# Narrower first weights, their zero subtraction moved into the first block, and their loads put elsewhere

## The chip, the cores and the metric

The kernel runs on one core of a Trainium2 chip. The metric is the device time of one launch in microseconds. A profiled execution gives, beside its time, a trace of every instruction on the engines: TensorE (PE, with its weight loads, PEld, shown apart), VectorE (DVE), ScalarE (ACT) and GpSimd (POOL), and of the DMA queues that SyncE (SP), ACT and POOL fill. Instructions of one engine start in its program order, so one that waits holds up all those behind it.

## The reference

One layer of cross attention and a feed-forward network with weights of integers, for 32 batches of 64 rows of 512 values:

```python
x = x + xattn(layernorm(x), ctx, ctx, Wq, bq, Wk, bk, Wv, bv, Wo, bo)
x = x + ffn(layernorm(x), gate_w, gate_z, gate_s, up_w, up_z, up_s, down_w, down_z, down_s)

def dequantize(imatrix, scales, zeros, group_size, out_dtype):
    rs = jnp.repeat(scales, group_size, axis=0)
    rz = jnp.repeat(zeros, group_size, axis=0)
    return ((imatrix.astype(rs.dtype) - rz.astype(rs.dtype)) * rs).astype(out_dtype)
gate = jax.nn.silu(jnp.dot(x, gate_proj))
up = jnp.dot(x, up_proj)
return jnp.dot(gate * up, down_proj)
```

The attention mixes the 64 rows of a batch (8 heads of 64 columns each, a softmax over 64 scores). The feed-forward network goes from 512 to 1792 columns (gate and up) and back to 512 (down). Its weights are integers from 0 to 15, with a zero and a scale for each group of 128 input rows and each column.

## The kernel before, in words

Two batches make a pair of 128 rows. There are 16 pairs, four to a block, so four blocks of 512 rows. Attention runs on pairs, the feed-forward network on a whole block with the 512 rows as the moving side of each product. Each operand of the feed-forward products is split into a high and a low part (`hTh` and `hTl` for the input, `hh` and `hl` for the hidden values), so that each weight tile is used twice.

**The weights.** `ng`, `nu` and `nd` hold gate, up and down in SBUF for the whole run. They are loaded as 32-bit values by DMAs that POOL issues (`load_wide`, line 265, for gate and up; `load_down`, line 269). Then the zeros are subtracted in place. For gate and up POOL does it with one instruction for each group g of 128 rows (line 302), for down VectorE does it for each 128 rows (line 308). The result is the integers that the products take; scales are applied to the products. The zeros reach SBUF in two steps: `zeros_to_dram` writes them in narrow types to DRAM, and `load_zeros` (line 279) reads them back, copied to all 128 partitions, by three DMAs that SP issues (two for `z16`, which holds gate's and up's zeros, one for `z8`, down's). `z16` and `z8` exist once each, so the load for one chunk has to wait until the subtractions of the chunk before are done.

All this is done in chunks of columns, listed in `wide` (line 166): 512, 512, 512 and 256 of the 1792. `weight_steps` (line 293) is a generator that makes one subtraction at each step, in the order of chunks, and within a chunk first gate and up by turns for g = 0 to 3, then down. It is advanced from two places: four times by the word `integers` in the first block's list, and then a few times in each round of the main loop.

**The first block.** Attention for pairs 0 to 3 is ordered by hand: the string `START` (line 741) lists steps, `0.turn` for the step `turn` of pair 0 and so on, and each engine takes its instructions in this order. The steps of a pair are: `stats`, `scale`, `apply` (layer norm: VectorE, POOL, VectorE), `k`, `q`, `v` and their `_out` forms, `scores`, `highest`, `less`, `exp`, `sums`, `divide` (the softmax; `divide` is POOL's), `turn` and `turn_out` (weights times Wo), `weigh` and `residual` (the attention's output added to x, on VectorE, and x stored), `stats2`, `scale2`, `apply2` (the second layer norm; `scale2` is POOL's), `flip`, `high`, `low` (transposed, then split in `hTh` by ScalarE and `hTl` by VectorE). Words without a number are other work: `gate`, `up` and `down` load the first chunk's weights, `zeros` writes the zeros to DRAM, `broadcast` reads the first chunk's zeros back, `rows` loads the next pairs' x, `quotients` makes ratios of scales (`s_inv`, `s_q`, on VectorE). `behind_products` (line 781) makes the first instruction of what it encloses wait for the TensorE instruction that stands last at that point of the list.

**The main loop** (line 864) goes in 28 rounds for each block. In each round two lanes, one for even and one for odd tiles f of 128 hidden columns, take a step of `gate_up` (line 595: two products for gate and two for up, for one g of one f), `down` of an earlier f takes two steps from round 6 on, and attention of the next block takes a step. Tile f of the first block needs its chunk's integers: f = 0 starts in round 0, f = 1 in round 2, f = 2 in round 4, and so on. Loads of later chunks are issued in rounds 0, 5 and 13 (line 884).

Of the kernel before, what the change touches and what calls it, by code (L numbers as in the profile page):

```python
# [9 lines left out]
F32 = mybir.dt.float32  # L10
F32R = mybir.dt.float32r
I32 = mybir.dt.int32
U8 = mybir.dt.uint8
BF16 = mybir.dt.bfloat16
AF = mybir.ActivationFunctionType
ALU = mybir.AluOpType
# [10 lines left out]
def kernel(  # L27
# [41 lines left out]
    nc = tc.nc  # L69
    B, D, L = x.shape  # L70
    I = gate_w.shape[1]
    P = 128
    NH, HD = 8, L // 8
    KT = L // P
# [16 lines left out]
    z8_dram = dram.tile([FC * L], U8, name="z8_dram")  # L91
# [22 lines left out]
    with ExitStack() as fast:  # L114
        const = fast.enter_context(tc.tile_pool(name="const", bufs=1))
        rows = fast.enter_context(tc.tile_pool(name="rows", bufs=1))
        att = fast.enter_context(tc.tile_pool(name="att", bufs=1))
        blk = fast.enter_context(tc.tile_pool(name="blk", bufs=2))
        zeros = fast.enter_context(tc.tile_pool(name="zeros", bufs=1))
# [43 lines left out]
        bqk = bias[:, : 2 * D].rearrange("p (m d) -> p m d", m=2)  # L163
        bvo = bias[:, 2 * D :]
        CW = 512
        wide = [(c, min(CW, I - c)) for c in range(0, I, CW)]
        w_T = const.tile([P, 4, D], F32, tag="w_T", name="w_T")
        WK, WV, WQ, WO = range(4)

# [95 lines left out]
        def load_wide(w: bass.AP, src: bass.AP, at: int, n: int):  # L265

            newest["POOL"] = nc.gpsimd.dma_start(w[:, :, at : at + n], src[:, :, at : at + n]).ins

        def load_down(at: int, n: int):
            fs = slice(at // P, (at + n) // P)  # L270
            newest["POOL"] = nc.gpsimd.dma_start(nd[:, fs, :], down_rows[:, fs, :]).ins

        def load_weights(at: int, n: int):

            load_wide(ng, gate_rows, at, n)
            load_wide(nu, up_rows, at, n)
            load_down(at, n)

        def load_zeros(at: int, n: int):
            z16 = zeros.tile([P, 2, KT, CW], BF16, tag="z16", name=f"z16_{at}")  # L280
            z8 = zeros.tile([P, KT, CW], U8, tag="z8", name=f"z8_{at}")
            for m in range(2):
                nc.sync.dma_start(
                    z16[:, m, :, :n], z_rows[m, :, at : at + n].partition_broadcast(P)
                )
            nf = n // P
            zd = z8_dram[at // P * L : (at // P + nf) * L]
            nc.sync.dma_start(
                z8[:, :nf, :].rearrange("p f l -> p (f l)"), zd.partition_broadcast(P)
            )  # L290
            return z16, z8

        def weight_steps(zs):

            for i, (at, n) in enumerate(wide):
                if i:
                    zs = load_zeros(at, n)
                z16, z8 = zs
                for g in range(KT):
                    for m, dst in enumerate((ng, nu)):  # L300
                        piece = dst[:, g, at : at + n]
                        nc.gpsimd.tensor_tensor(  # L302
                            piece, piece.bitcast(F32), z16[:, m, g, :n], ALU.subtract
                        )
                        yield
                for i in range(n // P):
                    piece = nd[:, at // P + i, :]
                    nc.vector.tensor_tensor(piece, piece.bitcast(F32), z8[:, i, :], ALU.subtract)
                    yield
# [424 lines left out]
        def chain(*gens):  # L734
# [6 lines left out]
        START = """  # L741
            0.stats 0.scale 0.apply 1.stats projections 1.scale biases
            projections_out 1.apply 2.stats 0.k biases_out 2.scale 3.stats 0.q 1.q
            0.k_out 3.scale 0.q_out 1.k gate zeros 1.q_out 0.scores 1.k_out 2.k
            3.apply 1.scores broadcast 0.highest 2.apply 2.k_out 0.less 0.v
            1.highest 0.exp 2.q 1.less 0.v_out 3.q 0.sums 1.exp 2.v 2.q_out 0.divide
            3.k up 2.v_out 1.sums 2.scores 3.q_out 1.divide 3.k_out 1.v 2.highest
            3.scores 1.v_out 2.less 1.turn 3.highest 2.exp 0.turn rows 3.less
            1.turn_out 2.sums 3.exp 1.weigh 0.turn_out 3.sums 2.divide 3.v
            1.residual 1.stats2 3.divide 0.weigh 3.v_out 2.turn 0.residual 0.stats2  # L750
            1.scale2 3.turn down 2.turn_out 2.weigh 3.turn_out 1.apply2 0.scale2
            scales 2.residual 2.stats2 3.weigh scales_out 1.flip 3.residual 3.stats2
            2.scale2 1.high 0.apply2 3.scale2 integers integers integers integers
            2.apply2 0.flip 1.low 2.flip 3.apply2 0.high quotients 3.flip 2.high
            0.low 3.high 2.low 3.low
        """
        place = places(att)
        with (
# [9 lines left out]
            for p in range(PB):  # L768
                j, i = divmod(p, SET)
# [6 lines left out]

            def first_banks(name: str):
                return ps0.tile([P, 2, CW], F32, tag="s", name=name)

            @contextmanager  # L780
            def behind_products():
# [19 lines left out]
            for step in START.split():  # L801
                if step[0].isdigit():
                    getattr(pairs[int(step[0])], step[2:])()
                elif step == "gate":
                    load_wide(ng, gate_rows, *wide[0])
                elif step == "zeros":
                    zeros_to_dram()
                elif step == "broadcast":
                    with behind_products():
                        weights = weight_steps(load_zeros(*wide[0]))  # L810
                elif step == "up":
                    with behind_products():
                        load_wide(nu, up_rows, *wide[0])
                elif step == "rows":
                    with behind_products():
                        load_rows(PB // SET)
                elif step == "down":
                    with behind_products():
                        load_down(*wide[0])
                elif step == "integers":  # L820
                    next(weights)
                elif step == "quotients":
                    quotients()
                elif step.endswith("_out"):
                    next(halves[step[:-4]], None)
                else:
                    halves[step] = {
                        "projections": lambda: projections(w_nat),
                        "biases": lambda: biases(b_nat),
                        "scales": lambda: scales(s_nat),  # L830
                    }[step]()
                    next(halves[step])
# [30 lines left out]
        with ExitStack():  # L863
            for r in range(NBLK * ROUNDS + LAG):
# [16 lines left out]
                with ExitStack() as behind:  # L881
                    for ins in newest.values():
                        behind.enter_context(tc.issue_after(ins))
                    if r in (0, 5, 13):
                        load_weights(*wide[(0, 5, 13).index(r) + 1])
                    if r < ROUNDS:
                        advance(weights, 2 if r < 4 else 1 + r % 2)
                    else:
                        advance(tops, 1 + (r % 4 == 3))
                    if k in FINISH_AT or k + 2 in FINISH_AT:  # L890
                        advance(finishing)
# [120 lines left out]
```

## Time and profile before

| | us |
|---|---|
| median of 3 runs | 457.89 |
| lowest and highest of them | 454.89, 458.46 |
| the profiled execution, its time | 457.63 |
| the profiled execution, its span in the trace | 455.3 |
| TensorE busy in the span | 413.0 |
| VectorE busy | 330.5 |
| ScalarE busy | 309.3 |
| POOL busy | 280.4 |
| first product of the feed-forward part begins at | 43.85 |

Times within the trace are counted from the start of the span. The profile has several views: busy time of each engine in given stretches ("windows"), the instructions of one engine in order of time (its "timeline"; the columns are start, duration, engine, line, operation, output and inputs, shapes, and in square brackets the idle time before it with what ended it), the chain of waits that ends last, and the packets of the DMA queues in a stretch. Queue q0 holds what POOL issues, q1 what SP issues, q8 and q14 the engines' own instructions. "Issue" as a releaser means that nothing in the profile explains the wait.

### The profile page before, as it was taken

How to read it: one execution, taken by the hardware profiler on the slowest of the kernel's cores; microseconds unless marked ns; L12 is line 12 of the kernel's file. 1: busy time of each engine (PE TensorE's matmuls, PEld its weight loads, DVE VectorE, ACT ScalarE, POOL GpSimd, SP SyncE). 2: the span in 40 equal slices, each digit the busy share in tenths (PEclk: the TensorE clock that was granted, in tenths of full speed). 3: DMA queues.
4: the chain of work that ended last, by engine and by line, in shares of the span. 5: the costliest groups of instructions: out<-in, count | busy, mean ns of one | idle time of the engine just before them, and what ended most of it. 6: DMA issues, size and time to landing. Idle time of an engine off the chain costs nothing.

```text
span 455.3 us, 10322 instructions
## 1 busy us (share of the span) xinstructions
PE 413.0 (91%) x4175; PEld 315.3 (69%) x4175; DVE 330.5 (73%) x510; ACT 309.3 (68%) x473; POOL 280.4 (62%) x293
## 2 busy tenths in 40 slices
PE   4854998998999999999999899999999999999991
PEld 4642564766677776777778577786778888887870
DVE  5959553797979983696869775586869655668672
ACT  2332489665787669686788569785688788777750
POOL 5335749658474487676787676664566887883311
PEclk9988799999999999999999999999999999999996
DMA  6677959436102020141000012130001012100004
GB/s 205 204 246 229 254 188 273 118 100 183 53 26 74 2 93 1 45 141 50 1 23 25 2 48 94 48 94 1 1 1 48 1 47 94 46 1 0 1 2 145
DMA packets 20928, 36.55 MB, mean 80 GB/s; under 512 B 1848, under 2 KB 7432, under 8 KB 20872
## 3 DMA queue, kind: packets, MB, share of 16 engines
q1 hardware_dynamic: 14056, 24.20, 16.2%
q0 software_dynamic: 6208, 11.01, 8.8%
q8 instruction: 35, 0.57, 0.5%
q10 hardware_dynamic: 608, 0.59, 0.4%
q14 instruction: 21, 0.17, 0.1%
HBM read 27.37 MB, written 8.42 MB: 79 GB/s over the span
## 4 chain that ended last, share of the span: by engine, by line
PE 45%; POOL 23%; issue 15%; DVE 10%; ACT 4%; DMA 1%; ACTq 0%; POOLq 0%; DVEq 0%
PE pg L604 11%; PE pu L604 11%; PE pd L649 6%; POOL hl L631 6%; PE pd L652 5%; POOL squares L325 4%; POOL squares L323 4%; POOL hh L630 3%; DVE xn_set L112 2%; DVE y L660 2%; POOL nu L302 2%; POOL q_e_set L488 1%; POOL ng L302 1%; DVE k_eT_set L411 1%; DMA w_nat<-in_L_xattn_Wo_dram 1%
## 5 line engine op out<-in xcount | busy, mean ns | idle before, releaser
L660 DVE SCALAR_TENSOR_TENSOR y<-pd,s_all,y 128x512 f32<-128x512 f32 x204 | 150.1, 743 | 47.6 <-PE pd L652 45.1
L614 ACT ACTIVATE pg<-pg,s_q 128x512 f32<-128x512 f32 x168 | 111.5, 665 | 76.4 <-PE pg L604 75.0
L614 ACT ACTIVATE pu<-pu,s_q 128x512 f32<-128x512 f32 x168 | 110.7, 659 | 4.5 <-PE pu L604 4.4
L604 PE MATMUL pg<-hTh,ng 128*128 128x512 f32 x224 | 91.3, 407 | 6.3 <-POOL nu L302 2.9
L649 PE MATMUL pd<-hh,nd 128*128 128x512 f32 x224 | 93.9, 419 | 1.6 <-DVE y L660 1.1
L630 POOL CAST hh<-h 128x512 fp32r<-128x512 f32 x55 | 35.0, 636 | 93.0 <-DVE h L620 91.2
L604 PE MATMUL pu<-hTh,nu 128*128 128x512 f32 x224 | 90.6, 404 | 0.9 <-POOL nu L302 0.5
L604 PE MATMUL pu<-hTl,nu 128*128 128x512 f32 x224 | 89.3, 399 | 0.0
L604 PE MATMUL pg<-hTl,ng 128*128 128x512 f32 x224 | 89.2, 398 | 0.0
L652 PE MATMUL pd<-hl,nd 128*128 128x512 f32 x224 | 88.7, 397 | 0.0
L631 POOL TENSOR_TENSOR hl<-h,hh 128x512 fp32r<-128x512 f32 x55 | 72.0, 1310 | 4.4
L620 DVE SCALAR_TENSOR_TENSOR h<-pu,s_all,g 128x512 f32<-128x512 f32 x56 | 41.8, 746 | 34.2 <-ACT g L617 27.8
L325 POOL TENSOR_TENSOR squares<-squares 128x512 f32<-128x512 f32 (+1 forms) x46 | 55.1, 1197 | 1.7
L604 PEld LDWEIGHTS pg<-hTh,ng 128*128 128x128 f32 x224 | 42.2, 188 | 20.1 <-ACT pg L614 4.2
L649 PEld LDWEIGHTS pd<-hh,nd 128*128 128x128 f32 x224 | 42.0, 188 | 18.0 <-DVE y L660 4.9
L604 PEld LDWEIGHTS pu<-hTh,nu 128*128 128x128 f32 x224 | 42.3, 189 | 14.0 <-ACT pu L614 2.7
L604 PEld LDWEIGHTS pu<-hTl,nu 128*128 128x128 f32 x224 | 42.3, 189 | 9.7 <-issue 0.4
L604 PEld LDWEIGHTS pg<-hTl,ng 128*128 128x128 f32 x224 | 42.4, 189 | 9.1
L617 ACT ACTIVATE g<-pg,s_all 128x512 f32<-128x512 f32 x56 | 38.7, 692 | 13.9 <-PE pg L604 12.2
L652 PEld LDWEIGHTS pd<-hl,nd 128*128 128x128 f32 x224 | 42.2, 188 | 7.4
L302 POOL TENSOR_TENSOR ng<-ng,z 128x512 fp32r<-128x512 f32 (+1 forms) x16 | 17.0, 1060 | 8.1 <-DMA z<-z_dram 8.1
L302 POOL TENSOR_TENSOR nu<-nu,z 128x512 fp32r<-128x512 f32 (+1 forms) x16 | 17.2, 1072 | 0.0
(290 smaller groups left out, 480.0 us busy)
## 6 DMA issues: line engine op xcount, KB each, us to landing
ng<-in_L_ffn_gate_w_dram POOLq DMA_DIRECT2D x3, 1024.0 KB, 5.9
z<-z_dram SPq DMA_DIRECT2D x6, 512.0 KB
nu<-in_L_ffn_up_w_dram POOLq DMA_DIRECT2D x3, 1024.0 KB, 7.9
c_set<-in_ctx_dram SPq DMA_DIRECT2D x6, 512.0 KB
x<-in_x_dram SPq DMA_DIRECT2D x6, 512.0 KB
nd<-in_L_ffn_down_w_dram POOLq DMA_DIRECT2D x3, 1024.0 KB, 9.6
x_dram<-x SPq DMA_DIRECT2D x6, 512.0 KB
r<-x_dram SPq DMA_DIRECT2D x6, 512.0 KB
```

The costliest lines, as they stand in the source:

```text
L302: nc.gpsimd.tensor_tensor(piece, piece.bitcast(F32), z16[:, m, g, :n], ALU.subtract)
L323: nc.gpsimd.tensor_tensor(square[:, :n], piece, piece, ALU.mult)
L325: nc.gpsimd.tensor_tensor(total[:, :n], total[:, :n], square[:, :n], ALU.add)
L604: nc.tensor.matmul(acc, w[:, g, ts(f, P)], half[:, g, :], start=(g == 0 and half is hi), stop=(g == KT - 1 and half is lo), skip_group_che ...
L614: nc.scalar.activation(acc, acc, AF.Copy, scale=by)
L617: nc.scalar.activation(g_sb, acc, AF.Silu, scale=by)
L620: ins = nc.vector.scalar_tensor_tensor(h_sb, acc, by, g_sb, ALU.mult, ALU.mult)
L630: nc.gpsimd.tensor_copy(hh, h_sb)
L631: ins = nc.gpsimd.tensor_tensor(hl, h_sb, hh.bitcast(F32), ALU.subtract)
L649: nc.tensor.matmul(pd, w, h_hi[t, f], start=(t, f) != LAST, stop=False, skip_group_check=True)
L652: nc.tensor.matmul(pd, w, h_lo[t, f], start=False, stop=True, skip_group_check=True)
L660: ins = nc.vector.scalar_tensor_tensor(y, pd, by, y, ALU.mult, ALU.add)
```

## The change

The first chunk is 256 columns in place of 512, and the narrow chunk is no longer the last; there are still four. All eight subtractions of gate and up for this first chunk are made within the first block's list (eight words `integers` in place of four), gate's four first and then up's, four of them behind pair 3's `divide` and the other four among the `scale2` steps of POOL. The zeros of the first two chunks have buffers of their own (`early_zeros`, one of them from the pool `early`) and are loaded in the list; down's zeros are split off into `load_down_zeros`.

The loads stand elsewhere. The first load of gate moves from behind `1.k` to behind `3.k`, and waits for these products. The first load of up moves from behind `3.k` to behind `0.turn`, beside `rows`. The load of down leaves its place. New words load the second chunk: `more` its zeros (behind pair 3's `turn`), `more_gate` its gate weights (behind pair 1's `scale2`), `more_up` its up weights and down's weights for both chunks (behind pair 3's `scale2`). The main loop then loads the third chunk in round 5 and the fourth in round 13.

```diff
         CW = 512
-        wide = [(c, min(CW, I - c)) for c in range(0, I, CW)]
+        FIRST = 256
+        wide = [(0, FIRST)] + [(c, CW) for c in range(FIRST, I, CW)]
...
-        def load_zeros(at: int, n: int):
-            z16 = zeros.tile([P, 2, KT, CW], BF16, tag="z16", name=f"z16_{at}")
-            z8 = zeros.tile([P, KT, CW], U8, tag="z8", name=f"z8_{at}")
+        def load_zeros(at: int, n: int, pool=zeros):
+
+            z16 = pool.tile([P, 2, KT, n], BF16, tag="z16", name=f"z16_{at}")
             for m in range(2):
-                nc.sync.dma_start(
-                    z16[:, m, :, :n], z_rows[m, :, at : at + n].partition_broadcast(P)
-                )
...
+                nc.sync.dma_start(z16[:, m], z_rows[m, :, at : at + n].partition_broadcast(P))
+            return z16
+
+        def load_down_zeros(at: int, n: int):
+            z8 = zeros.tile([P, KT, CW], U8, tag="z8", name=f"z8_{at}")[:, : n // P, :]
+            zd = z8_dram[at // P * L : (at + n) // P * L]
+            nc.sync.dma_start(z8.rearrange("p f l -> p (f l)"), zd.partition_broadcast(P))
+            return z8
+
+        def weight_steps():
+
+            for at, n in wide:
+                z16 = early_zeros.pop(0) if early_zeros else load_zeros(at, n)
+                z8 = load_down_zeros(at, n)
+                pieces = [(m, g) for g in range(KT) for m in range(2)]
+                for m, g in pieces if at else sorted(pieces):
+                    piece = (ng, nu)[m][:, g, at : at + n]
+                    nc.gpsimd.tensor_tensor(
+                        piece, piece.bitcast(F32), z16[:, m, g, :], ALU.subtract
+                    )
+                    yield
...
-            0.k_out 3.scale 0.q_out 1.k gate zeros 1.q_out 0.scores 1.k_out 2.k
-            3.apply 1.scores broadcast 0.highest 2.apply 2.k_out 0.less 0.v
-            1.highest 0.exp 2.q 1.less 0.v_out 3.q 0.sums 1.exp 2.v 2.q_out 0.divide
-            3.k up 2.v_out 1.sums 2.scores 3.q_out 1.divide 3.k_out 1.v 2.highest
-            3.scores 1.v_out 2.less 1.turn 3.highest 2.exp 0.turn rows 3.less
-            1.turn_out 2.sums 3.exp 1.weigh 0.turn_out 3.sums 2.divide 3.v
-            1.residual 1.stats2 3.divide 0.weigh 3.v_out 2.turn 0.residual 0.stats2
-            1.scale2 3.turn down 2.turn_out 2.weigh 3.turn_out 1.apply2 0.scale2
-            scales 2.residual 2.stats2 3.weigh scales_out 1.flip 3.residual 3.stats2
-            2.scale2 1.high 0.apply2 3.scale2 integers integers integers integers
-            2.apply2 0.flip 1.low 2.flip 3.apply2 0.high quotients 3.flip 2.high
-            0.low 3.high 2.low 3.low
+            0.k_out 3.scale 0.q_out 1.k zeros 1.q_out 0.scores 1.k_out 2.k 3.apply
+            1.scores broadcast 0.highest 2.apply 2.k_out 0.less 0.v 1.highest 0.exp
+            2.q 1.less 0.v_out 3.q 0.sums 1.exp 2.v 2.q_out 0.divide 3.k gate
+            2.v_out 1.sums 2.scores 3.q_out 1.divide 3.k_out 1.v 2.highest 3.scores
+            1.v_out 2.less 1.turn 3.highest 2.exp 0.turn up rows 3.less 1.turn_out
+            2.sums 3.exp 1.weigh 0.turn_out 3.sums 2.divide 3.v 1.residual 1.stats2
+            3.divide integers integers integers integers 0.weigh 3.v_out 2.turn
+            0.residual 0.stats2 1.scale2 more_gate integers 3.turn more 2.turn_out
+            2.weigh 3.turn_out 1.apply2 0.scale2 integers integers scales 2.residual
+            2.stats2 3.weigh scales_out 1.flip 3.residual 3.stats2 2.scale2 integers
+            1.high 0.apply2 3.scale2 more_up 2.apply2 0.flip 1.low 2.flip 3.apply2
+            0.high quotients 3.flip 2.high 0.low 3.high 2.low 3.low
...
+                elif step == "more":
+                    with behind_products():
+                        early_zeros.append(load_zeros(*wide[1]))
+                elif step == "more_gate":
+                    load_wide(ng, gate_rows, *wide[1])
+                elif step == "more_up":
+                    load_wide(nu, up_rows, *wide[1])
+                    load_down(0, wide[1][0] + wide[1][1])
...
-                    if r in (0, 5, 13):
-                        load_weights(*wide[(0, 5, 13).index(r) + 1])
+                    if r in (5, 13):
+                        load_weights(*wide[(5, 13).index(r) + 2])
```

## The prediction, made before the changed kernel had run

> **What bounds the kernel now.** I read the windows of 100 us first. From 120 to 400 us TensorE is busy 77.53 of 80, 97.50 of 100 and 99.05 of 100 us: it is the bound there, and the change takes no matrix product away. The tail (after 435 us) is untouched too. So only the first 100 us can move the time, and there the start, up to the first product of the feed-forward part at 43.85 us, counts one for one, since everything behind it is shifted as a block. The chain of waits, in order of time, shows the hole in it:
>
> ```profile
> 22.10 0.57 PE pe L497 x23
> 22.67 5.15 issue
> 27.82 0.50 PE pe L497 x9
> ...
> 42.97 0.88 issue
> 43.85 0.70 PE pg L604 x2
> ```
>
> `pe` is pair 0's "turn", 32 matmuls with one wait at their head. They break off after 23 and resume 5.15 us later, with no semaphore to wait for ("issue"). What can be missing in the middle of such a run is the instructions. The DMA queues of the second 25 to 26 us (packets, MB, time as a share of the engines) show a block of them landing, between data:
>
> ```profile
> q0 software_dynamic: 150, 0.31, 92.7%
> q1 hardware_dynamic: 36, 0.07, 22.1%
> q8 instruction: 1, 0.02, 6.0%
> ```
>
> The other blocks of q8 before 50 us fall in seconds 11, 16, 28, 32 and 47, each without such a hole. What stood in front of the late one is read from SP's and POOL's timelines: zeros 1.25 MB issued from 17.24 us, up's weights 1 MB from 19.23, the next context 0.5 MB at 20.81. The windows of 2 us give 230 to 392 GB/s from 22 to 28 us.
>
> After the hole VectorE works without a gap until the feed-forward part can start, and its last `hTl` ends 0.1 us before the first `pg` at 43.85 (POOL's fourth subtraction ended at 42.96, so the label POOL on that wait is not the last releaser):
>
> ```profile
> 29.24 0.88 DVE L525 SCALAR_TENSOR_TENSOR x<-po,bias,x 128x256 f32<-128x256 f32 x2 [4.34 <-PE po L513]
> ...
> 33.08 0.54 DVE L112 TENSOR_SCALAR xn_set<-x,mv,rs 128x512 f32<-128x512 f32 x1
> ...
> 38.88 0.84 DVE L112 TENSOR_SCALAR xn_set<-x,mv,rs 128x512 f32<-128x512 f32 x1
> 39.64 1.19 DVE L236 SCALAR_TENSOR_TENSOR s_inv<-s_all 128x84 f32<-128x84 f32 x1
> ...
> 41.87 1.87 DVE L550 TENSOR_TENSOR hTl<-ph,hTh 128x512 fp32r<-128x512 f32 x3
> ```
>
> The 4.34 us of VectorE before 29.24 is all that the hole costs the path, since VectorE had work until 24.89 us. From 44 to 90 us TensorE is busy about nine tenths; ScalarE has no gap from 62.11 to 80.6 us (its timeline, with three table loads of 1.28 us), and POOL waits once, 8.05 us, for zeros (62.82 us).
>
> [...] `xn_set` takes 0.54 us alone and 0.84 beside POOL's subtractions, `s_inv` 1.19 us for 84 columns. [...] Here the clock is 0.50 from 46 to 50 us, and a product takes 0.79 us there against a mean of 0.41.
>
> **The change part by part.** Durations are from the rows above; the zero of the sum is the profiled execution, 457.63 us with a span of 455.3.
>
> *Transfers ahead of the hole.* Gate's first megabyte at 11.08 goes; half of it now stands where up's stood (behind pair 3's k products, 18.4 us). Zeros before the hole shrink from 1.25 to 0.5 MB. From 17.2 to 22.7 us 1.5 MB are queued in place of 2.75. At the 0.3 MB per us of these windows they are through 5 us after the first bytes at 18.5, so at 23.5, and not at 28. [...] I take the hole from 5.15 to 1.0 us; bounds 0 and, if it goes with bytes outstanding at its end, 3.
>
> *VectorE.* It is free at 24.89, so a hole of 0.8 us or less costs nothing more: its residual sums start at 25.1 in place of 29.24, gain 4.1.
>
> *POOL in the start.* Four subtractions of 128x512 (38.28 to 42.96, mean 1.17) become eight of 128x256; that shape has a row, 0.67 us. Four of gate stand after the divisions of pairs 2 and 3, which end at 26.32: 26.5 to 29.2. The `scale2` of pair 1 stands behind them, 29.2 to 29.75. VectorE wants it for its first `xn_set`, 3.84 us after its residual sums began, at 28.95: loss 0.8. Then come the issue of gate's next megabyte (0.82), one subtraction of up (0.67) and pair 0's `scale2`, done at 31.8, wanted at about 34: covered. The remaining three are between `scale2` steps 2 us apart: covered, 0; if up's 0.5 MB are late they are not (rival). From the first `xn_set` VectorE ran 10.66 us to its last `hTl`; POOL is now quieter beside `s_inv`, which I put at 0.4 (nearest: 0.37 for the multiply of the same 84 columns), and `xn_set` at 0.54: 1.1 less, bounds 0 and 1.3. So 29.8 + 9.55 + 0.1 = 39.45 for the first product, a gain of 4.4; with 0.25 for the divisions, now queued behind up's issue that waits for pair 0's turn, 4.15.
>
> *Later loads.* Gate, up (1 MB each), down (1.5 MB) and 1 MB of zeros move from 47 us and later to 28 to 36 us: with x, the stores and the rest some 6.6 MB from 26 us, at 0.35 MB per us until about 46. POOL issues are 0.8 us each, after its last `scale2`: nothing waits. VectorE's subtractions from `nd` stand before the bias addition of q, wanted 13 us after the first product (56.80 − 43.85), so at 52: down's weights have 6 us to spare. Covered, 0; bounds −1 and +3 (VectorE in order behind a late load). The later chunk loads are now 1 MB where the last was half; POOL then waits for zeros before chunk 3's first subtraction, ahead of two splits of `h`. `pd` of f=3 runs at 90.33 and its split ended at 83.57: 6.8 us of cover.
>
> *44 to 90 us.* POOL's wait of 8.05 us goes, and two subtractions fewer (2.4 us) stand ahead of the division of pairs 4 and 5. But ScalarE is full from 62 to 81 us, so most of it is hidden. TensorE's only wait for POOL there is 1.33 us at 74.5. I take a gain of 0.5; bounds −2 (the cold clock falls otherwise) and +3 (both the 1.33 and half of the cold stretch go).
>
> Sum: 4.15 + 0.5 = 4.65, so 457.63 − 4.65 = **453.0 us**. The median of the runs, 457.89, is 0.3 above the profiled one, and the three spread from 454.89 to 458.46: 1% (4.6 us) is about what a measurement here tells from no change.
>
> **Rivals.**
> 1. The hole moves or only halves. For: the next block is fetched just when up, x and the zeros now start[...]. Against: between 28 and 30 us the queues carried 67 GB/s. Then the start gains 2 and the time is 455.6.
> 2. Slower. POOL's in-order queue: up's first subtraction waits for a load issued only after pair 0's turn, and three `scale2` steps stand behind it. If the hole stays at 5 us, up is issued at 28.3 and the divisions of pairs 2 and 3 wait behind that issue (24.28 to 29.1); with the 6 to 9 us that up's loads took to land it is there at 35 to 38, and pairs 0, 2 and 3 scale at 36 to 41 in place of 33.3 to 38.4. First product 2 to 4 us later, and the 3.5 MB behind it run into VectorE's `nd` for some 2 more: about 462. It decides when up lands later than about 36 us; before 31.5 it costs nothing.
> 3. Faster by more: `s_inv`, POOL and the cold stretch all give. Products from 44.8 to 51.6 us run at half clock; sparing half of that is 2, with the 1.33 of POOL 3 more: 450.0.
> That the weights' work in all stays the same (32 subtractions of POOL, of the same bytes) speaks against any effect after 100 us.
>
> **How the numbers follow.** The forecast 453.0 (451.3 to 455) has 0.45, rival 1 0.20, rival 2 0.15, rival 3 0.20. The bound for "faster" is 453.3; the forecast lies below it in 0.6 of its cases: 0.27 + 0.20 = 0.47. Slower by over 1% (above 462.5) is half of rival 2 and what I can't see, 0.12; the rest, 0.41, is within 1%. For 8 in 10 the range runs from 449.3 to 457.6: it leaves out rival 2 and the end of rival 3.
>
> **What would show it.** Right: pair 0's turn in one piece or with a hole of about 1 us; VectorE's residual sums at about 25 us; the first `pg` at about 39.5, and the same distance kept at 100 us. Wrong: another "issue" hole of over 2 us on TensorE before 50 us; POOL waiting for DMA at `nu` before its `scale2`; VectorE waiting for a DMA at `nd`; the first `pg` early and the gain gone by 100 us.

## The result, and the profile after

| | before | after |
|---|---|---|
| median of 20 runs each, us | 457.88 | 458.14 |
| lowest and highest | 454.89, 459.22 | 455.48, 462.41 |
| the profiled execution, its span | 455.3 | 458.8 |
| first product of the feed-forward part begins at | 43.85 | 39.50 |

The ratio is 1.002, with a 95% interval from 0.9997 to 1.0044: no change, where 453.0 was forecast. The profiled execution of after took 460.93 us, 2.8 above the median, so its trace shows somewhat more loss than a usual run has.

The start went as forecast. TensorE's timeline after (start, duration, engine, line, what; idle time before it in brackets) has pair 0's turn in one piece, and the first `pg` is 4.35 us earlier:

```profile
22.38 0.69 PE L496 MATMUL pe<-w_T,q_e_set 64*64 64x64 f32 x32 [0.16 <-PE pe L496]
...
39.50 0.77 PE L603 MATMUL pg<-hTh,ng 128*128 128x512 f32 x1 [1.62 <-issue]
```

The third block on q8 after 10 us, the one that landed in second 25 of before, lands in second 19 here. The DMA queues of that second (packets, MB, share of the engines' time) show it alone:

```profile
q8 instruction: 1, 0.02, 7.4%
```

The first zeros, 0.5 MB, were issued at 14.66 us (17.24 in before) and had passed by then. Gate's 0.5 MB, issued at 19.51, moved nothing before 21 us. So the block did not come early through a queue of 1.5 MB, as the prediction had it: it came between two loads.

VectorE's timeline of after shows the steps to it, and directly behind them the first loss:

```profile
25.10 0.82 DVE L524 SCALAR_TENSOR_TENSOR x<-po,bias,x 128x256 f32<-128x256 f32 x2
...
29.68 0.98 DVE L112 TENSOR_SCALAR xn_set<-x,mv,rs 128x512 f32<-128x512 f32 x1 [0.70 <-POOL rs L380]
...
36.38 0.24 DVE L237 SCALAR_TENSOR_TENSOR s_inv<-s_all 128x84 f32<-128x84 f32 x1
...
37.52 1.88 DVE L549 TENSOR_TENSOR hTl<-ph,hTh 128x512 fp32r<-128x512 f32 x3
...
45.27 0.69 DVE L374 BATCH_NORM_STATS2 st_6to<-x 128x6 f32<-128x512 f32 x1 [4.59 <-DMA x<-in_x_dram]
45.88 0.17 DVE L375 BATCH_NORM_AGGREGATE mv_4to<-st_4to 128x2 f32<-128x6 f32 x1
```

`st_6to` is the first statistic of pairs 6 and 7, which nobody needs yet. But it stands in VectorE's order between the two `mv_4to` of pairs 4 and 5, so the second of these starts at 45.88, behind the 4.59 us that VectorE waits for this x. In before it stood behind all of this, and its x was there (VectorE's timeline of before):

```profile
46.19 0.15 DVE L377 TENSOR_SCALAR rs_4to<-mv_4to 128x2 f32<-128x2 f32 x1
46.26 0.68 DVE L375 BATCH_NORM_STATS2 st_6to<-x 128x6 f32<-128x512 f32 x1
```

In after, behind the second `mv_4to`, POOL's `rs_4to` and four subtractions wait in order (POOL's timeline), and so does TensorE's `pv_4to` (its own):

```profile
46.84 0.72 POOL L380 TENSOR_TENSOR rs_4to<-rs_4to,nhalf 128x2 f32<-128x2 f32 x1 [9.90 <-DVE mv_6to L375]
```

```profile
51.45 1.99 PE L433 MATMUL pv_4to<-c_set,w_T 64*64 64x256 f32 x16 [4.28 <-DVE k_eT_set L410]
```

The second loss lies from 95 to 140 us. In windows of 1 us of after TensorE runs dry at 100 us, and then comes back at half clock (0.50). The columns are the window's length, the busy us (and count of instructions) of TensorE, its weight loads, VectorE, ScalarE and POOL, then the granted clock, the DMA share and GB/s:

```profile
99.00:100.00 1.00, 0.46 (x2) 0.03 (x1) 1.00 (x2) 0.50 (x1) 1.00 (x2) 1.00 0.00 0
100.00:101.00 1.00, 0.00 (x0) 0.00 (x0) 1.00 (x1) 0.19 (x1) 1.00 (x3) 1.00 0.22 20
101.00:102.00 1.00, 0.13 (x1) 0.13 (x1) 1.00 (x3) 0.00 (x0) 1.00 (x2) 0.81 0.69 94
102.00:103.00 1.00, 1.00 (x3) 0.81 (x4) 1.00 (x2) 0.00 (x0) 0.85 (x1) 0.50 1.14 371
103.00:104.00 1.00, 1.00 (x7) 0.35 (x9) 1.00 (x2) 0.02 (x1) 0.00 (x0) 0.50 1.28 424
104.00:105.00 1.00, 1.00 (x41) 1.00 (x44) 1.00 (x3) 0.65 (x1) 0.00 (x0) 0.50 1.26 408
```

Three timelines of after, of VectorE, of TensorE and of POOL, show what meets there. (`pg`, `pu` and `pd` are TensorE's products with gate, up and down; `h` is made of the first two, and VectorE sums the `pd` in `y`.)

```profile
98.14 3.03 DVE L112 TENSOR_SCALAR xn_set<-x,mv_6to,rs_6to 128x512 f32<-128x512 f32 x2
```

```profile
101.87 0.79 PE L648 MATMUL pd<-hh,nd 128*128 128x512 f32 x1 [2.41 <-DVE y L659]
...
136.39 0.50 PE L603 MATMUL pu<-hTh,nu 128*128 128x512 f32 x1 [2.06 <-POOL nu L301]
```

```profile
99.33 0.84 POOL L268 DMA_DIRECT2D ng<-in_L_ffn_gate_w_dram  x1
100.16 0.75 POOL L268 DMA_DIRECT2D nu<-in_L_ffn_up_w_dram  x1
100.89 0.76 POOL L272 DMA_DIRECT2D nd<-in_L_ffn_down_w_dram  x1
101.65 1.20 POOL L301 TENSOR_TENSOR nu<-nu,z 128x512 fp32r<-128x512 f32 x1
111.15 0.61 POOL L629 CAST hh<-h 128x512 fp32r<-128x512 f32 x1 [8.30 <-PE pg L603]
```

The subtraction at 101.65 is the last one of the third chunk, and tile 6 needs it. In before, tile 6 belonged to the second chunk, whose last subtraction ended at 84.7, and `xn_set` of pairs 6 and 7 stood behind the `h` of tile 6 (timelines of before, of POOL and of VectorE):

```profile
83.53 1.16 POOL L302 TENSOR_TENSOR nu<-nu,z 128x512 fp32r<-128x512 f32 x1
```

```profile
101.46 0.73 DVE L620 SCALAR_TENSOR_TENSOR h<-pu,s_all,g 128x512 f32<-128x512 f32 x1
...
102.78 2.60 DVE L112 TENSOR_SCALAR xn_set<-x,mv_6to,rs_6to 128x512 f32<-128x512 f32 x1
```

The edge of each chunk has moved up by two tiles, which is four rounds. By the counts of steps in each round (two in rounds 0 to 3, then one and two by turns), the last subtraction of the second, third and fourth chunk fell in rounds 9, 17 and 25; now it falls in 5, 13 and 21. The three DMA issues of the next chunks stayed in rounds 5 and 13, 2.35 us of POOL directly ahead of it. The order of TensorE's program followed: tile 6's last two `pu` stand behind products of tiles 5, 7 and 8, so TensorE has nothing to do while its `pd` waits for `y`, which waits for VectorE's `xn_set`.

From here on a kernel's lead is the time by which the `h` of a tile, or the first `pd` of a tile, comes earlier than in before. Leads are in us and of the one profiled execution, which can lie off the kernel's median: 2.8 us above it in after, 3.5 above in steps_earlier, 1.8 below in stats_behind. So read a lead along its row. Medians are of all runs of a kernel, 6 to 22 here; before, run beside each series, had medians of 457.15 to 457.88.

| kernel | h, tile 0 | h, tile 5 | h, tile 6 | pd, tile 8 | pd, tile 9 | last h | median |
|---|---|---|---|---|---|---|---|
| after | 2.22 | 1.48 | −8.87 | −2.12 | −4.44 | −3.45 | 458.14 |
| after_again | 4.50 | 3.57 | −6.96 | −0.22 | −4.06 | −3.05 | 457.24 |
| stats_behind | 8.26 | 7.28 | −3.06 | 3.68 | 1.36 | 2.44 | 456.24 |
| fourth_chunk_later | 7.46 | 6.79 | 2.83 | 4.27 | 3.96 | 4.92 | 453.80 |
| apply_behind | 7.34 | 6.05 | −1.84 | 3.32 | 3.02 | 4.17 | 454.14 |
| steps_earlier | 4.22 | 4.76 | 4.16 | 5.31 | 5.31 | 6.67 | 446.95 |
| stats_and_steps | 8.04 | 7.89 | 7.29 | 8.47 | 8.47 | 9.81 | 446.51 |
| up_after_turn | 2.00 | 1.99 | 1.99 | 1.98 | 1.98 | 1.96 | 455.46 |

### The profile page after: what moved, and what is told of

Same layout as the page of the kernel before. It is cut to its first block, busy times and chain, and to the rows that moved or that the text cites. A ratio compares the mean times of both kernels' runs of the same rounds, so it can differ in the third digit from the quotient of the medians.

```text
span 458.8 us, 10320 instructions
## 1 busy us (share of the span) xinstructions
PE 414.8 (90%) x4175; PEld 315.7 (69%) x4175; DVE 329.2 (72%) x510; ACT 309.7 (67%) x473; POOL 281.3 (61%) x292
## 4 chain that ended last, share of the span: by engine, by line
PE 44%; POOL 22%; issue 12%; DVE 12%; DMA 6%; ACT 2%; POOLq 0%; SPq 0%; DVEq 0%
PE pu L603 12%; PE pg L603 11%; PE pd L648 7%; POOL hl L630 6%; PE pd L651 5%; POOL squares L324 4%; POOL squares L322 4%; DMA x<-in_x_dram 3%; POOL hh L629 3%; DVE xn_set L112 3%; DMA z<-z_dram 2%; DVE y L659 2%; DVE k_eT_set L410 1%; POOL ng L301 1%; POOL q_e_set L487 1%
```

## The experiments

**The hole alone.** The kernel before, with up's first load behind pair 0's turn:

```diff
-            3.k up 2.v_out 1.sums 2.scores 3.q_out 1.divide 3.k_out 1.v 2.highest
+            3.k 2.v_out 1.sums 2.scores 3.q_out 1.divide 3.k_out 1.v 2.highest
...
-            3.scores 1.v_out 2.less 1.turn 3.highest 2.exp 0.turn rows 3.less
+            3.scores 1.v_out 2.less 1.turn 3.highest 2.exp 0.turn up rows 3.less
```

> The kernel before, with one word of its list moved: up's first weights (1 MB, POOL's issue) stand behind pair 0's turn and no longer behind pair 3's k. Theory 1 (TensorE's hole of 5.15 us in pair 0's turn is a block of instructions held up by the data that is in flight): with 1 MB of 2.75 less ahead of it the hole shrinks to 2 us or less, and VectorE's residual sums start by 26.5 in place of 29.24; the first pg comes earlier by up to 3 us unless up's weights are then late for POOL's subtractions. Theory 2 (the hole is something else, or only the zeros of 1.25 MB count): it stays at 4 us or more.

Its TensorE timeline:

```profile
22.00 0.57 PE L497 MATMUL pe<-w_T,q_e_set 64*64 64x64 f32 x23 [0.16 <-PE pe L497]
25.80 0.50 PE L497 MATMUL pe<-w_T,q_e_set 64*64 64x64 f32 x9 [3.23 <-issue]
```

One megabyte less ahead of the break takes 1.92 us from it (5.15 to 3.23). The hole that is left lies between the theories: under the 4 us or more of theory 2, over the 2 us or less of theory 1. The 1.25 MB of zeros still stand ahead of it here: from 20 to 28 us the queues carry 1.56 MB of SP's and two blocks on q8, and nothing of q0, up's queue (in before the block lands in second 25, where most of the data are up's weights). No run takes the zeros alone away. The first `pg` comes 1.9 us earlier, and in the table its lead is the same 2.0 at every tile to the end. Ratio to before 0.995 (0.9929 to 0.9972). So the start counts one for one here, and what after wins there it must lose elsewhere.

**The first loss.** After, with the statistics of pairs 6 and 7 held behind what VectorE has been given:

```diff
-                        getattr(sets[j], what)()
+                        with ExitStack() as behind:
+                            if (t, i, what) == (1, 1, "stats"):
+                                behind.enter_context(tc.issue_after(newest["DVE"]))
+                            getattr(sets[j], what)()
```

> The kernel after, but the first layer-norm statistics of pairs 6 and 7 (VectorE, 45.27 us, 4.59 us of waiting for their x) are held behind the work that VectorE has been given by then, so that the scale of pairs 4 and 5 no longer stands behind the late x. Theory 1 (the start's gain is lost because VectorE waits in order for x of pairs 6 and 7): the wait of 4.59 us is gone or stands later and shorter, POOL's rs_4to starts at about 42.5 in place of 46.84, TensorE's 4.28 us before pv_4to at 51.45 shrink below 1, pv_4to starts at 46.5 to 47.5, and the median is 3 to 4 us below that of after (about 454.5). Theory 2 (the lateness of the transfers only changes its place: the next instruction in order, the subtraction from nd or the late x itself, holds VectorE as long): pv_4to starts at 50 or later and the time is that of after within 1 us. Theory 3 (a later loss at 95 to 115 us eats it): pv_4to is early as in theory 1, and the lead is gone at pd of tile 6.

TensorE's and VectorE's timelines:

```profile
46.56 1.09 PE L433 MATMUL pv_4to<-c_set,w_T 64*64 64x256 f32 x16
```

```profile
50.66 1.29 DVE L307 TENSOR_TENSOR nd<-nd,z 128x512 fp32r<-128x512 f32 x2 [4.60 <-DMA nd<-in_L_ffn_down_w_dram]
```

The chain is as theory 1 has it: `pv_4to` at 46.56 with no wait, and a lead of 8.26 us at tile 0. VectorE now waits as long for `nd`, but what stands behind `nd` is not yet wanted. Of that lead 5.8 us are gone at the end: theory 3 holds too. The median gains 1.9, half of the 3 to 4 expected. That is near the noise: the ratio to before is 0.9986 (0.9968 to 1.0004), and against the second series of after, next, the gain is 1.0. The second series also shows one reason why it is not more.

**The same kernel again.**

> The kernel after, unchanged, to see how much of its first trace is the execution's own: that one was 460.93 us, 2.8 above its median of 458.14. If the landing of x of pairs 6 and 7 (45.25 us there, 42.6 and 43.3 in two kernels that are the same up to that point) varies from one execution to the next, VectorE's wait at st_6to is 2 to 3 us here in place of 4.59, pv_4to starts 2 to 3 us earlier, h of tile 0 stands 4 to 7 us ahead of before in place of 2.22, and the loss between tiles 5 and 9 is the same, about 5 us. If the first trace was typical, x lands at 45 again and h of tile 0 stands 2 us ahead.

The median was 457.24 (0.9984 to 1.0028 of before). VectorE waited 3.36 us for x, and tile 0 had a lead of 4.50. In eight traces, of after and of kernels whose edits come later than this, `st_6to` begins at 42.37 to 45.27 us after a wait of 2.2 to 4.6: the landing varies with the execution, and the first trace was the worst of them. The loss between tiles 5 and 9 is there again, 7.6 us (3.57 + 4.06; 5.9 in the first trace).

**Why x is late.** After, with 2.5 MB of the second chunk (`more_up`) issued in the main loop's first round:

```diff
-            1.high 0.apply2 3.scale2 more_up 2.apply2 0.flip 1.low 2.flip 3.apply2
+            1.high 0.apply2 3.scale2 2.apply2 0.flip 1.low 2.flip 3.apply2
...
+                    if r == 0:
+                        load_wide(nu, up_rows, *wide[1])
+                        load_down(0, wide[1][0] + wide[1][1])
```

> The kernel after, but the second chunk's up weights (1 MB) and down's weights of the first two chunks (1.5 MB), which stood in the first block behind pair 3's scale2, are issued in the first round of the main loop. Theory 1 (x of pairs 6 and 7 is late because 2.5 MB more are in flight beside it): x lands by about 41 in place of 45.25, VectorE's wait at st_6to is under 1 us; but down's weights then land later, so the gain of 3 to 4 us shows only if the subtractions from nd, behind rs_4to and k_eT_set in VectorE's order, don't wait in turn. If they do, by 2 to 4 us, the time is that of after within 1 us. Theory 2 (x is late for another reason, the SP queue's own issue or its small share whatever is beside it): the wait at st_6to stays above 3 us.

`st_6to` began at 43.31 after a wait of 2.13 us, within the spread of the unchanged start, and the median was 457.13 (0.9972 to 1.0024 of before). This neither shows nor rules out that these loads delay x; it does not cure it.

**The second loss.** After, with the fourth chunk issued two rounds later, and, in another run, both chunks one round later:

```diff
-                    if r in (5, 13):
-                        load_weights(*wide[(5, 13).index(r) + 2])
+                    if r in (5, 15):
+                        load_weights(*wide[(5, 15).index(r) + 2])
```

> The kernel after, but the fourth chunk's weights are issued by POOL in round 15 of the first block in place of round 13. Theory A (the loss at 95 to 105 us comes from VectorE's xn_set, 3.03 us instead of 2.60, which runs beside POOL's issues and delays y and with it TensorE's pd by 2.41 us): with the issues elsewhere the 2.41 us shrink by 0.4 or more and up to 2 us come back; pd of tile 6 is then no later than in before. Theory B (it is VectorE's order: one xn_set of any length stands ahead of y): TensorE's wait before that pd stays above 2 us and the time is that of after within 1 us. If the later loads make POOL's or VectorE's subtractions of that chunk wait, the time rises by 1 to 3.

TensorE's timeline of fourth_chunk_later:

```profile
95.43 0.50 PE L603 MATMUL pu<-hTh,nu 128*128 128x512 f32 x1 [1.26 <-POOL nu L301]
95.77 0.40 PE L603 MATMUL pu<-hTl,nu 128*128 128x512 f32 x1
96.37 0.50 PE L648 MATMUL pd<-hh,nd 128*128 128x512 f32 x1 [0.21 <-DVE y L659]
```

The median fell by 4.3 us (ratio to before 0.9923, 0.99 to 0.9946), more than theory A allowed. The issues are gone from beside `xn_set` (the first is at 101.37), and it still took 2.83 us (3.03 in after). So they are not what makes it long, as A had it. What changed is the order: tile 6's last `pu` are back in their place ahead of `pd`, and fill the time until `y` is there.

> The kernel after with one number changed twice: the third and fourth chunks are issued in rounds 6 and 14, one later than in after, so that POOL's three issues of 0.75 to 0.84 us (2.35 together) no longer stand directly ahead of the one subtraction that tile 2 (nu of the second chunk) and tile 6 (nu of the third) are waiting for, but directly behind it. Theory D (the later loss is these 2.35 us at the worst place: with a first chunk of 256 the last subtraction of each chunk falls into rounds 5, 13 and 21, and the issues stayed in 5 and 13): pu of tiles 2 and 6 comes before the next tile's, h of tile 6 keeps the lead of tile 5 to within 1 us, and the median is 4 to 5 us below after (453 to 454), as with the fourth chunk alone, or a little lower for tile 2. Theory E (the subtractions as such are too late, whatever stands ahead of them, so that two steps a round are needed): 456 or more.

With both issues directly behind the due subtractions (6 and 14 in place of 5 and 13) the median was 455.06 (0.9968, 0.9944 to 0.9991), 3.1 below after: near to D, and not all of it. Tile 6 still lost 4 us against tile 5 (leads 1.95 and 5.90), as it does in fourth_chunk_later (2.83 and 6.79); from there to the first `pd` of tile 9 that one gains 1.1 us, this one loses 0.9.

Next, the issues stay and `xn_set` moves: the edit of the first loss, with "apply" for "stats". `xn_set` of pairs 6 and 7 then stands behind all four `y` of tile 4. Nothing else changes its place on VectorE, ScalarE and POOL; on TensorE two products of gate and one of down move forward here.

> The kernel after, but VectorE's first layer-norm multiply of pairs 6 and 7 (xn_set, two instructions, 3.03 us together at 96 to 99 us) is held behind the work given to VectorE by then, so that it stands behind all four y of tile 4 and not ahead of the first; POOL's issues of the fourth chunk stay ahead of the third chunk's last nu subtraction. Theory A (the loss between tiles 5 and 9 is VectorE's xn_set making y and so pd late by 2.41 us, with the cold clock behind it): the 2.41 us go and 2 us or more come back, a median of 456 or lower. Theory D (the loss is tile 6's integers: their last subtraction stands behind 2.35 us of issues, and TensorE's last pair of pu of tile 6 falls behind the products of later tiles): the wait before pd is gone, but h of tile 6 is still 7 us or more later against before than h of tile 5 is, and the median is after's within 1 us.

It gave 454.14 (0.9928, 0.9907 to 0.995), against what D expected. In windows of its trace, TensorE has a gap again, but one that stays at full clock:

```profile
98.00:100.00 2.00, 0.75 (x4) 0.28 (x2) 2.00 (x4) 1.30 (x3) 0.28 (x1) 1.00 1.26 400
100.00:102.00 2.00, 1.97 (x20) 1.33 (x21) 2.00 (x4) 0.81 (x1) 0.00 (x0) 1.00 1.29 404
```

So neither A nor D alone is the cause: the stall of 2.41 us needs `pu` of tile 6 held back and `y` held back behind `xn_set`, and lifting either brings 3 to 4 us back. The table says where they come back. From `h` of tile 5 to `pd` of tile 8 after_again loses 3.8 us, fourth_chunk_later and apply_behind 2.5 and 2.7; from `pd` of tile 8 to that of tile 9 it loses 3.8, these two 0.3. The larger part thus falls at tile 10, whose `pu` runs between these `pd`. A wait of about 2 us for its `nu` is there in the traces of after, after_again, stats_behind, issues_next_round and stats_and_fourth, which all have a half-clock stretch (0.50) within 95 to 106 us, and not in these two, where the clock is 1.00 in every window of 1 us from 90 to 142 us. The two go together; that one causes the other is not shown.

**The steps earlier.** Two weight steps a round until round 12, the issues left in 5 and 13:

```diff
-                        advance(weights, 2 if r < 4 else 1 + r % 2)
+                        advance(weights, 2 if r < 12 else 1 + r % 2)
```

> The kernel after, but the weight steps go two a round until round 12 (in place of round 4, then one and two by turns), so that the third chunk's last subtraction of nu, which tile 6 needs, stands ahead of the fourth chunk's issues and not behind them; the issues stay in round 13. Theory B' (the loss from tile 5 to tile 9 comes from tile 6 now belonging to the third chunk: its integers are made in the very rounds in which it is multiplied): TensorE's products of tile 6 no longer fall behind those of tile 7, h of tile 6 is within 1 us of its lead at tile 5, and the median is 3 to 4 us below after's 458.14. Theory A (POOL's issues beside VectorE's xn_set make y late): the issues still stand there, so the wait before pd stays at 2 us or more and the time is after's within 1 us. Rival C: the earlier subtractions wait for the third chunk's zeros (issued only when they are due, some 10 us to land) and hold up POOL's splits of h by up to 8 us, as they do once in before; then it is slower than after.

POOL's timeline has tile 6's last subtraction ahead of the issues, by 8 us:

```profile
86.37 1.61 POOL L301 TENSOR_TENSOR nu<-nu,z 128x512 fp32r<-128x512 f32 x1
...
96.07 0.83 POOL L268 DMA_DIRECT2D ng<-in_L_ffn_gate_w_dram  x1
```

The median is 446.95, ratio to before 0.9778 (0.9746 to 0.981): 11.2 below after where 3 to 4 were expected. Its lead is kept from tile 5 to tile 9 and grows beyond, and TensorE is busy in all of 120 to 140 us (17.80 of 20 in after). The profiled execution, 450.48 us, was the slowest of the six; its lead of 6.67 at the last `h` is therefore less than the median's gain, and stats_and_steps (447.12, lead 9.81) shows better what a usual run has. Is that the repair, or would any kernel with this loop win by it? The same edit in before:

> A control: the kernel before with the same edit of the steps that brought after from 458 to 447 (two weight steps a round until round 12). If that gain is the repair of what the change broke (the due rounds of tiles 2, 6 and 10), before has little to win: in it the issues stand in the middle of a chunk's subtractions, and the time is 455 to 459. If two steps a round help any kernel with this loop (tiles 4, 8 and 12 are just as short of time in before), it comes to 452 or lower, and only the rest of the 11 us belongs to the change.

457.45 (1.0003, 0.9986 to 1.002): nothing. The gain comes only together with the changed chunks.

**The combinations.** Statistics behind, with the fourth chunk in round 15, and with the earlier steps; and both of these, statistics and earlier steps, with the loads issued in rounds 4 and 10 behind the steps of the round (the statistics are part of this edit too, though its text names the steps alone):

> The kernel after with both edits: the statistics of pairs 6 and 7 held behind VectorE's other work, and the fourth chunk issued in round 15. If the two losses are separate and add up, the lead of 8 us that the first alone shows at h of tile 0 and the 5 us that the second alone keeps at tile 9 stand together: pd of tile 9 is 6 us or more ahead of before and the median is 452 or lower (458.14 less 1.9 less 4.3 is 451.9). If one lead only fills slack that the other leaves (something in between, such as the third chunk's zeros, sets the pace), the median stays at 453 to 454.

> The kernel after with the statistics of pairs 6 and 7 held behind and two weight steps a round until round 12, the fourth chunk in round 13. Two steps a round alone gave 446.95. If the wait for x is a loss of its own, its 1.9 us (458.14 to 456.24 when done alone) come on top: 445 or lower. If the third chunk's loads and zeros, which POOL waits for at 73 and 78 us with the steps alone, set the pace from there on, the earlier start is eaten and the time is 446 to 448.

> The kernel after with two weight steps a round until round 12 and, beside that, the third and fourth chunks issued in rounds 4 and 10, behind the steps of the round and not ahead of them. With the steps alone (446.95) POOL still waits for the loads, 0.93 and 1.61 us at 73 and 78 us and 4.09 and 1.54 at 102 and 105. If these waits hold up TensorE (they stand ahead of splits of h), 1 to 2 us more come back: 445 to 446. If they lie beside other work, the time is that of the steps alone within 0.7. If the earlier loads collide with x, the context or the zeros of the same rounds, it is slower by 1 to 2.

They gave 452.20 (0.9897, 0.9868 to 0.9926), 446.51 (0.9772, 0.9744 to 0.9801) and 447.59 (0.979, 0.977 to 0.981). By the medians the two losses add up in the first (5.9 = 1.9 + 4.3 less 0.3). With the steps the wait for x is worth only 0.4 more, which six runs of each, 445.66 to 450.48 and 445.53 to 447.64, do not tell from nothing. The third belongs beside 446.51, from which it differs in the loads alone: 1.1 slower. So the earlier loads bring nothing, though POOL's waits for the fourth chunk's weights fall from 6.7 to 1.7 us: these lie beside other work. The kernel of 446.51 beats both before and after by over 11 us. Statistics behind, round 15 and the earlier steps cannot stand in one kernel: with two steps a round the fourth chunk's first subtraction falls in round 13, ahead of loads issued in round 15.

**Tile 10.** After with only the fourth chunk's steps earlier, and the same with `xn_set` moved:

```diff
-                        advance(weights, 2 if r < 4 else 1 + r % 2)
+                        advance(weights, 2 if r < 4 or r >= 14 else 1 + r % 2)
```

> The kernel after with two weight steps a round from round 14 on (rounds 0 to 3 as before, rounds 4 to 13 one and two by turns), so that only the fourth chunk's subtractions come earlier: its last nu stands ahead of the split of tile 9 and no longer ahead of that of tile 10. If tile 10 has a loss of its own (TensorE's 2.06 us before a pu at 136 us and the cold clock behind it), that wait is gone, pd of tile 9 no longer falls 2 to 4 us back against tile 8, and the median is 2 to 3.5 us below after's 458.14. If tile 10 only shows what tile 6 began, the loss stays and the time is after's within 1 us.

> The kernel after with VectorE's xn_set of pairs 6 and 7 behind the four y of tile 4 (alone 454.14) and two weight steps a round from round 14 on. If the losses at tiles 6 and 10 are separate, it is 451 to 452, the sum of both gains. If the second only fills what the first left, 453.5 to 454.5.

459.96 (1.0075, 1.0048 to 1.0101) and 458.24 (1.0031, 1.0014 to 1.0048): slower than without, by 1.8 and 4.1. The wait for `nu` at tile 10 is gone, and TensorE's timeline of the second one has another in its place, for POOL's division:

```profile
129.29 0.47 PE L496 MATMUL pe_6to<-w_T,q_e_set 64*64 64x64 f32 x2 [4.85 <-POOL q_e_set L487]
```

POOL's timeline of that run says why. It begins the fourth chunk only when the zeros are there, at 113 us, and then has eight subtractions ahead of the division:

```profile
113.05 2.29 POOL L301 TENSOR_TENSOR ng<-ng,z 128x512 fp32r<-128x512 f32 x2 [5.18 <-DMA z<-z_dram]
...
127.34 1.90 POOL L487 TENSOR_TENSOR q_e_set<-q_e_set,sm_6to 128x1024 f32<-128x1024 f32 x1
```

In steps_earlier, with the steps earlier from round 4 on, the zeros' one buffer is free when the third chunk is done, at 88 us; SP issues the next zeros at 88.00 (in this run at 103.47), POOL's first subtraction of the chunk is at 102.48 and the division at 120.72. That fits the earlier steps being worth more than a cure at tile 6: they move POOL's whole queue forward. So neither of these edits lifts a loss at tile 10 alone, and how the 7 us beyond the cure of tile 6 divide between tile 2, tile 10 and the division stays open.

## Why the prediction was wrong

- "Transfers ahead of the hole": with 1 MB less in flight ahead of it the hole was 1.92 us shorter (up_after_turn), which fits the prediction, but the way to 0 was not the one it reckoned. It had 1.5 MB through at 23.5 us and a hole of 1.0. In fact the zeros came 2.6 us earlier than in before, 0.5 MB ahead of the block at 19 us, with the queues empty behind it. SP waits 0.6 us for the write of the narrow zeros to DRAM; in before, with gate's first megabyte under way, it waits 4.1. The prediction did not see this, so that the hole is wholly gone is in part luck.
- "VectorE" and "POOL in the start": right. Sums of the residual at 25.10 (25.1), `scale2` of pair 1 at 29.08 (29.2), first `pg` at 39.50 (39.45). Two terms were off and nearly cancel: the first `xn_set` took 0.98 us, not 0.54, with POOL's issue of gate beside it, and `s_inv` took 0.24, not 0.4.
- "Later loads ... Covered, 0; bounds −1 and +3 (VectorE in order behind a late load)": this step failed. The mechanism stood in the bound, but the prediction weighed `nd` alone. It was x of pairs 6 and 7, whose first user stands ahead of its need in VectorE's order. The wait was 2.2 to 4.6 us in different executions; moving it is worth 1.0 to 1.9 by the medians. A slip of the sum beside it, 6.6 MB at 0.35 MB per us from 26 us, which ends at 45 and not 46, changes nothing.
- "POOL then waits for zeros before chunk 3's first subtraction ... 6.8 us of cover": the wait came (1.02 us at 82.42) and was covered; the lead at the first `pd` of tiles 2 and 3 is 0.79 both times.
- "So only the first 100 us can move the time" and "That the weights' work in all stays the same ... speaks against any effect after 100 us": the term after 100 us was put at nothing, and this is the step that cost most. The work is the same, but its due times are not: tiles 2, 6 and 10 are now the first of their chunks. With the issues and the pace of the steps left where they were, after loses 6 to 8 us between tiles 5 and 9, where steps_earlier gains 0.5.
- "44 to 90 us": a gain of 0.5 was too small. Where x does not hold VectorE, the lead grows from about 4.3 at the first `pg` to 8 at tile 0 (stats_behind, stats_and_steps). About half of that is the clock, by an estimate: from the first `pg` to tile 0's `h` it was 0.80 over 17.41 us in before and 0.88 over 13.73 in stats_behind, so 3.5 and 1.6 us were not granted. The reading of ScalarE there was also too full: between 62.11 and 80.6 us it has gaps of 0.21 and 0.24 and two table loads, not three.
- The rivals: the hole of the first did not come. Of the second, slower one nothing was seen: POOL's first subtraction of up, at 30.46 us, waited for no load. The third's gains before 60 us are in stats_behind's trace in part (the clock above), and are lost again behind it. None of them names a due time.

So the gain of the forecast was there, 4.35 at the start (up to 8 at tile 0 once x is out of the way), and was given back between 40 and 57 us and between 95 and 140. Of the signs named, the first `pg` early and the gain gone by 100 us came true in the first trace, where 0.6 us were left at tile 5's first `pd`, 107 us; in the second 2.5 were left there, and nothing at tile 8.

## What to carry to other kernels

When the edges of chunks move, the due time of every chunk moves with them. Lay the new due rounds beside whatever is pinned to a round number (loads, issues, the pace of a generator), even if the total work is unchanged. An instruction that waits for a load holds up what stands behind it in its engine's order (here VectorE's `st_6to`, 4.59 us), so look for the first user of every late transfer, not only of those that the change moves. And an edit that removes one wait (tile 10's) can make the kernel slower (by 1.8 us in steps_from_14), when the same queue then makes something else late (the division).

## What the runs showed of the hardware

TensorE's granted clock fell to 0.50 behind an idle time of 2.41 us at tile 6 in after, after_again and stats_behind. By windows of 1 us it stayed there for about 3.4 us: those of after give 0.81, then 0.50 three times, then 0.99 from 101 to 106 us. In steps_from_14, behind the same 2.41 us, products took 0.63 us in place of 0.39. At tile 10 an idle time of 2.05 us was followed by a stretch at 0.50 in after_again (136 to 138 us). Idle times of 2.06 us in after, 2.04 in stats_behind, 2.05 in issues_next_round and 1.93 in stats_and_fourth were not: there the clock is 1.00 in every window of 1 us from 128 to 142 us. So the cold clock that the expectation of steps_from_14 puts behind the 2.06 us is after_again's, not after's. A series of gaps of 1.25, 0.21 and 0.44 us within 4 us was followed by 0.50 in issues_next_round (99 to 102 us); nearly the same series (1.26, 0.21, 0.44) was not in fourth_chunk_later (1.00). What decides between the two is not shown by these traces. By an estimate from these figures such a stall costs its idle time alone or 1.7 us more (half of 3.4), as the clock falls or not; that may be one source of the spread between executions.

The break in TensorE's instructions was 5.15 us in before, where the block on q8 landed in second 25, behind the zeros' 1.25 MB and among up's 1 MB; 3.23 in up_after_turn, where SP's 1.56 MB passed from 20 to 28 us without up; and none in after, where the block landed in second 19 between two loads. That TensorE waited for this block is the author's reading: the profile calls the break "issue" and names no releaser.
